# A graph layer's first stage, regrouped: blocks of 1536 nodes, the third vector component in four row groups, destinations loaded from a pool of their own

## The chip, the cores and the metric

The kernel runs on one core of a Trainium2 chip. The metric is device microseconds for one execution; before the change the runs took 5697.79 us in the median of three (5664.32 to 5704.07). One further execution was profiled; it took 4345.69 us, and the span from its first to its last instruction is 4343.6 us. Every time read from a view below is of that execution.

## What is computed

There are N = 12500 nodes with 160 features each: 64 scalars `s` and 32 vectors `v` of 3 components. There are 400000 edges, sorted by destination. Cut to what matters:

```python
h_s = s @ lin1_ws * a / sqrt(64)                                   # first stage: h, one row of 160 per node
h_v = einsum('nci,cd->ndi', v, lin1_wv) * a / sqrt(32)
w = silu(edge_scalars @ fc_w1 / 8) @ fc_w2 / 8                     # 224 weights per edge
es, ev = h_s[edge_src], h_v[edge_src]                              # gather
mid = products of w, es, ev and edge_attr                          # per edge
agg = segment_sum(mid, edge_dst) / 4                               # per destination
pre = sc(s, v) * a + agg @ lin2 * a                                # self connection, output map
out = layernorm(x + gated(silu / sigmoid of pre))
```

## The kernel before, in words

The program has five parts; each of the engines TensorE (PE), VectorE (DVE), ScalarE (ACT) and GpSimd (POOL) works through its own list of instructions in order, and SP and ACT also issue DMAs, each in its order.

**Setup (lines 99 to 120).** ACT issues the loads of `at` (node_vec1, 128 nodes to a column), of the 64x64 weight `l1s` (line 102) and of `l1v`, a 96x96 block-diagonal matrix with `lin1_wv` three times (lines 106 to 115). DVE scales both (lines 103 and 112). POOL fills the accumulator `acc`, 96x25088 numbers, with zeros (line 119).

**First stage (lines 122 to 149).** It computes h for all nodes into a table in DRAM, `h_tab`. Chunks of 1024 nodes: SP loads `xs` (64 partitions, line 129) and `xv` (96 partitions, one group of 32 for each vector component, line 131), three buffers of each. For each tile of 128 nodes PE makes two products, line 136 with 64 and line 137 with 96 rows of contraction; the node features are the stationary operand (128 columns) and the weights are the moving one (64 or 96 columns). A float32 product is two weight loads and two matmuls. The result goes to one of six PSUM buffers `hp`. DVE (even tiles, line 142) or ACT (odd tiles, line 140) multiplies by `at` into `ht`, and SP writes eight tiles with one DMA (line 146; line 149 for the rest of 84 nodes). The write stands in SP's list among the loads of later chunks.

**Destinations (lines 155 to 179).** `db` (line 157) and `dt` (line 160), two layouts of all destinations of 1.6 MB each, are loaded by ACT's queue. DVE takes the smallest and largest destination of each block of 640 edges (lines 162 and 163), ACT's queue writes them to DRAM (165) and reads them back in two layouts, `both` (167) and `lo` (170). DVE subtracts `lo` from `dt` to give `rel` (171), which the selections of the main loop compare with a ramp, and makes `rows` and `again`. The tiles of this part lie in a pool "ends" that takes the memory that the pool "nodes" of the first stage gives back, so its loads come after that stage has let its buffers go.

**Main loop (line 348 and those that lines 354 to 520 call).** 3125 tiles of 128 edges, four to a step. POOL gathers the rows of h (line 260, one indirect DMA to a tile), PE computes the edge weights (251, 272), DVE the products (280, 289) and the selection matrices (299, 302), PE sums by destination (318), ACT and PE turn and map the sums (322 to 343) and DVE adds them to `acc` (348). PE, DVE, ACT and POOL keep the order in which the code is written there. SP's loads (`es` line 239, `idx` 369, `eat` 371) lie in a pool "loads", opened at the loop and placed in memory that "nodes" and "ends" have given back.

**Last stage (from line 565).** Gates, residual and layernorm of the 98 tiles.

Outside the main loop the framework puts each engine's instructions into an order of its own, by what is ready and by the place in the code; the small weights of lines 195 to 231 (ACT's queue, some 50 loads) are spread in this way over the first stage. All DMAs share eight semaphores in turn.

Of the kernel before, what the change touches and what calls it, by code (L numbers as in the profile page):

```python
# [10 lines left out]
F32 = mybir.dt.float32  # L11
I32 = mybir.dt.int32
# [3 lines left out]
OP = mybir.AluOpType  # L16
AX = mybir.AxisListType
ENG = mybir.EngineType
PSUM = bass.MemoryType.PSUM

P = 128
S = 64
V = 32
V3 = 3 * V
D = S + V3
TB = 5
BG = 25
EB = TB * P
EG = BG * EB
W = 32  # L30
# [31 lines left out]
def gnn_kernel(  # L62
# [21 lines left out]
    nc = tc.nc  # L84
    N = x.shape[0]
    NT = attr.shape[1]
    NP = NT * P
    G = src.shape[0]
    NB = G * BG
# [3 lines left out]
    consts = ctx.enter_context(tc.tile_pool(name="consts", bufs=1))  # L93
    dram = ctx.enter_context(tc.tile_pool(name="dram", bufs=1, space=bass.MemoryType.DRAM))
    h_tab = dram.tile([N, D], F32, name="h_tab")
    bounds = dram.tile([2, NB], I32, name="bounds")


    at = consts.tile([P, NT], F32, name="at")
    nc.scalar.dma_start(at, attr)  # L100
    l1s = consts.tile([S, S], F32, name="l1s")
    nc.scalar.dma_start(l1s, lin1_ws)
    nc.vector.tensor_scalar_mul(l1s, l1s, 1.0 / math.sqrt(S))

    def block_diagonal(name, w, n, scale):
        k = w.shape[0]
        m = consts.tile([n * k, n * k], F32, name=name)
        nc.vector.memset(m, 0.0)
        for i in range(n):
            nc.scalar.dma_start(m[i * k:(i + 1) * k, i * k:(i + 1) * k], w)  # L110
        if scale != 1.0:
            nc.vector.tensor_scalar_mul(m, m, scale)
        return m

    l1v = block_diagonal("l1v", lin1_wv, 3, 1.0 / math.sqrt(V))


    acc = consts.tile([V3, 2, NP], F32, name="acc")
    nc.gpsimd.memset(acc, 0.0)


    with tc.tile_pool(name="nodes", bufs=3) as nodes, tc.tile_pool(
        name="nodes_ps", bufs=6, space=PSUM
    ) as nps:
        CH = 1024
        for c0 in range(0, N, CH):
            cn = min(CH, N - c0)
            xs = nodes.tile([S, CH], F32, name="xs")
            nc.sync.dma_start(xs[:, :cn], xs_t[:, c0:c0 + cn])
            xv = nodes.tile([V3, CH], F32, name="xv")  # L130
            nc.sync.dma_start(xv[:, :cn], xv_t[:, c0:c0 + cn])
            ht = nodes.tile([P, CH // P, D], F32, name="ht")
            for q in range(0, cn, P):
                n = min(P, cn - q)
                p = nps.tile([P, D], F32, name="hp")
                nc.tensor.matmul(p[:n, :S], xs[:, q:q + n], l1s, start=True, stop=True)
                nc.tensor.matmul(p[:n, S:], xv[:, q:q + n], l1v, start=True, stop=True)
                t = (c0 + q) // P
                if t % 2:
                    nc.scalar.mul(ht[:n, q // P], p[:n], at[:n, t:t + 1])  # L140
                else:
                    nc.vector.tensor_scalar(ht[:n, q // P], p[:n], at[:n, t:t + 1], None,
                                            op0=OP.mult)
            full = cn // P
            if full:
                nc.sync.dma_start(
                    h_tab[c0:c0 + full * P, :].rearrange("(q p) d -> p q d", p=P), ht[:, :full])
            if cn > full * P:
                nc.sync.dma_start(h_tab[c0 + full * P:c0 + cn, :], ht[:cn - full * P, full])


    rel = consts.tile([P, NB * TB], I16, name="rel")
    rows = consts.tile([1, NB], I32, name="rows")
    again = consts.tile([1, 1], I32, name="again")
    with tc.tile_pool(name="ends", bufs=1) as ends:
        db = ends.tile([G * BG // 5, 5, EB], I32, name="db")
        nc.scalar.dma_start(db.rearrange("a b e -> a (b e)"),
                            dst_b.rearrange("g (a e) -> (g a) e", e=5 * EB))
        dt = ends.tile([P, NB, TB], I32, name="dt")
        nc.scalar.dma_start(dt.rearrange("p b t -> p (b t)"), dst)  # L160
        mm = ends.tile([G * BG // 5, 2, 5], I32, name="mm")
        nc.vector.tensor_reduce(mm[:, 0], db, AX.X, OP.min)
        nc.vector.tensor_reduce(mm[:, 1], db, AX.X, OP.max)
        for k in range(2):
            nc.scalar.dma_start(bounds[k].rearrange("(a b) -> a b", b=5), mm[:, k])
        both = ends.tile([1, 2, NB], I32, name="both")
        nc.scalar.dma_start(both.rearrange("o k b -> o (k b)"),
                            bounds.rearrange("(o k) b -> o (k b)", o=1))
        lo = ends.tile([P, NB], I32, name="lo")
        nc.scalar.dma_start(lo, bounds[0:1, :].to_broadcast([P, NB]))  # L170
        nc.vector.tensor_tensor(rel.rearrange("p (b t) -> p b t", t=TB), dt,
                                lo[:, :, None].to_broadcast([P, NB, TB]), op=OP.subtract)

        nc.vector.tensor_copy(rows, both[:, 0])
        wide = ends.tile([1, NB], F32, name="wide")
        nc.vector.tensor_sub(wide, both[:, 1], both[:, 0])
        widest = ends.tile([1, 1], F32, name="widest")
        nc.vector.tensor_reduce(widest, wide, AX.X, OP.max)
        nc.vector.tensor_scalar(again, widest, float(W), float(G), op0=OP.is_ge, op1=OP.mult)


    ident = consts.tile([P, P], F32, name="ident")
# [14 lines left out]
    for half in range(2):  # L197
        r = slice(half * S, (half + 1) * S)
# [25 lines left out]
    for to, part, pieces, w, r0, c0, by in maps:  # L224
        for k, piece in enumerate(pieces):
# [3 lines left out]
            r = l2[at_r:at_r + V, m, c0:c0 + w.shape[1]]  # L229
# [124 lines left out]
            out.append([(half, u) for half in range(2) for u in range(t, t + 2) if u < sides[half]])  # L354
        return out

    with tc.tile_pool(name="loads", bufs=2) as loads, tc.tile_pool(
        name="edge", bufs=2
    ) as edge, tc.tile_pool(name="deep", bufs=4) as deep, tc.tile_pool(
        name="pw_ps", bufs=2, space=PSUM  # L360
    ) as pw_ps, tc.tile_pool(name="pa_ps", bufs=2, space=PSUM) as pa_ps, tc.tile_pool(
        name="misc_ps", bufs=2, space=PSUM
# [54 lines left out]
        for n, (_, _, tiles) in enumerate(steps):  # L417
            for t, _, _ in tiles:
                b = t // TB
# [110 lines left out]
        with tc.For_i(0, n_again, 1) as g, tc.For_i(0, BG, 1) as k:  # L530
            b = g * BG + k
# [4 lines left out]
            ends = loads.tile([1, 2], I32, name="ends1", bufs=1)  # L536
# [10 lines left out]
            r = edge.tile([P, TB], F32, name="r", bufs=1)  # L547
# [17 lines left out]
    with tc.tile_pool(name="fin", bufs=2) as fin, tc.tile_pool(  # L565
        name="fin_ps", bufs=4, space=PSUM
    ) as fps:
        full = N // P
# [3 lines left out]
        for t0, nt, p in groups:  # L572
# [5 lines left out]
            for t in range(nt):  # L578
                c = (t0 + t) * P
                a = at[:p, t0 + t:t0 + t + 1]  # L580
                pp = fps.tile([P, 2, V3], F32, name="pp")
                for k in range(2):
# [4 lines left out]
                                               op0=OP.mult, op1=OP.mult)  # L587
# [11 lines left out]
            for t in range(nt):  # L599
                nc.vector.tensor_scalar(y[:p, t], y[:p, t], mv[:p, t, 0:1], rs[:p, t:t + 1],  # L600
                                        op0=OP.subtract, op1=OP.mult)
# [47 lines left out]
```

## Time and profile before

| what | value |
|---|---|
| runs, median of three | 5697.79 us |
| profiled execution | 4345.69 us, span 4343.6 us |
| PE busy / DVE / ACT / POOL in the span | 3481.0 / 2620.0 / 749.0 / 3083.3 us |
| first matmul of the first stage | 21.85 us after the start |
| last product of the first stage ends | about 134.8 us |
| issue of the load of `db` | 137.49 us |
| first gather | 176.69 us |
| last gather | about 4190 us |

The profile gives, for each engine, what it did and when; "idle before" names the thing that ended a wait. A busy share is an average over stages with different limits, so the parts are read one by one, with the window of each. The profiled execution is shorter than the timed ones by 1352 us; a change of some us in one stage is worked out in the profiled execution and then set beside the median.

### The profile page before, as it was taken

How to read it: one execution, taken by the hardware profiler on the slowest of the kernel's cores; microseconds unless marked ns; L12 is line 12 of the kernel's file. 1: busy time of each engine (PE TensorE's matmuls, PEld its weight loads, DVE VectorE, ACT ScalarE, POOL GpSimd, SP SyncE). 2: the span in 40 equal slices, each digit the busy share in tenths (PEclk: the TensorE clock that was granted, in tenths of full speed). 3: DMA queues.
4: the chain of work that ended last, by engine and by line, in shares of the span. 5: the costliest groups of instructions: out<-in, count | busy, mean ns of one | idle time of the engine just before them, and what ended most of it. 6: DMA issues, size and time to landing. Idle time of an engine off the chain costs nothing. (4 is left out here: it accounts for less than half of the span.)

```text
span 4343.6 us, 90044 instructions
## 1 busy us (share of the span) xinstructions
PE 3481.0 (80%) x36179; PEld 2014.9 (46%) x36179; DVE 2620.0 (60%) x5738; ACT 749.0 (17%) x1662; POOL 3083.3 (71%) x3133
## 2 busy tenths in 40 slices
PE   6588888888888887788888888888878888888873
PEld 6344444444444444444444444444444444444442
DVE  3356666656666665666656566566656665566659
ACT  1111111111111111111111111111111111111124
POOL 2277777777777777777777777777777777777740
PEclk9999999999999999999999899999999999999975
DMA  4434433433334343433444333443443433433324
GB/s 113 124 91 102 95 92 93 101 91 94 95 91 100 94 95 91 101 95 89 96 99 94 91 95 92 97 97 93 96 98 92 96 93 94 99 93 88 92 74 118
DMA packets 231236, 416.33 MB, mean 96 GB/s; under 512 B 63556, under 2 KB 158544, under 8 KB 230561
## 3 DMA queue, kind: packets, MB, share of 16 engines
q0 software_dynamic: 150000, 256.20, 25.2%
q1 hardware_dynamic: 77622, 150.43, 13.8%
q8 instruction: 284, 4.65, 0.5%
q10 hardware_dynamic: 3192, 3.92, 0.4%
q14 instruction: 138, 1.13, 0.1%
HBM read 394.31 MB, written 16.00 MB: 94 GB/s over the span
## 5 line engine op out<-in xcount | busy, mean ns | idle before, releaser
L260 POOL DMA_INDIRECT hg<-h_tab,idx x3125 | 3061.5, 980 | 1105.9 <-issue 881.6
L318 PE MATMUL pa<-pr,sel 128*32 128x192 f32 x25000 | 1339.5, 355 | 548.3 <-DVE pr L289 543.0
L280 DVE TENSOR_TENSOR pr<-pw,hg 128x512 f32<-128x512 f32 x782 | 539.5, 690 | 1526.0 <-DMA hg<-h_tab,idx 1339.5
L318 PEld LDWEIGHTS pa<-pr,sel 128*32 128x32 f32 x25000 | 759.5, 116 | 997.5 <-DVE pr L289 676.8
L289 DVE TENSOR_TENSOR pr<-pw,hg 128x384 f32<-128x384 f32 x2346 | 1158.1, 549 | 10.5 <-issue 6.0
L272 PE MATMUL pw<-w,hid 64*128 64x224 f32 x6250 | 849.5, 392 | 0.7 <-ACT hid L253 0.7
L272 PEld LDWEIGHTS pw<-w,hid 64*128 64x128 f32 x6250 | 563.3, 197 | 440.4 <-issue 346.9
L302 DVE TENSOR_TENSOR sel<-oh,eat 128x640 f32<-128x640 f32 x625 | 517.3, 828 | 44.0 <-DVE oh L299 0.9
L251 PE MATMUL ph<-es,w 128*128 128x512 f32 x940 | 496.4, 612 | 44.6 <-DMA idx<-in_src_dram 40.8
L253 ACT ACTIVATE hid<-ph 128x512 f32<-128x512 f32 (+1 forms) x470 | 246.7, 525 | 962.4 <-PE ph L251 962.4
L322 ACT COPY sa<-pa 128x384 f32<-128x384 f32 x313 | 149.5, 478 | 1418.1 <-PE pa L318 1415.2
L339 PE MATMUL po<-tt,l 96*96 96x256 f32 (+1 forms) x1738 | 391.2, 381 | 0.0
L330 PE MATMUL pt<-ident,sa 128*96 128x128 f32 x1250 | 265.3, 294 | 148.3 <-ACT tt L331 148.3
L339 PEld LDWEIGHTS po<-tt,l 96*96 96x96 f32 x1738 | 275.4, 163 | 104.8 <-issue 22.4
L331 ACT COPY tt<-pt 96x256 f32<-96x256 f32 x626 | 229.8, 367 | 384.8 <-PE pt L330 383.3
L330 PEld LDWEIGHTS pt<-ident,sa 128*96 128x96 f32 x1250 | 107.6, 126 | 314.5 <-ACT tt L331 227.3
L251 PEld LDWEIGHTS ph<-es,w 128*128 128x128 f32 x940 | 151.1, 202 | 206.1 <-issue 181.7
L299 DVE TENSOR_TENSOR oh<-rel,iota 128x160 f32<-128x160 int16 x625 | 196.5, 314 | 0.0
L343 ACT COPY os<-po 96x512 f32<-96x512 f32 (+1 forms) x79 | 45.5, 577 | 599.2 <-PE po L339 599.2
L348 DVE TENSOR_TENSOR acc<-acc,os 96x64 f32 x625 | 133.3, 213 | 12.9 <-ACT os L343 7.9
L583 PE MATMUL pp<-ident,acc 96*128 96x96 f32 x196 | 53.0, 379 | 70.8 <-DVE y L588 37.1
L309 PE MATMUL pa<-none 1*128 1x384 bf16 x313 | 107.6, 344 | 0.0
(54 smaller groups left out, 681.9 us busy)
## 6 DMA issues: line engine op xcount, KB each, us to landing
es<-in_es_t_dram SPq DMA_DIRECT2D x312, 320.0 KB
hg<-h_tab,idx POOLq DMA_INDIRECT x3125
h_tab<-ht SPq DMA_DIRECT2D x12, 640.0 KB
xt<-in_x_dram SPq DMA_DIRECT2D x7, 1040.0 KB
out_dram<-y SPq DMA_DIRECT2D x7, 1040.0 KB
eat<-in_ea_dram SPq DMA_DIRECT2D x25, 250.0 KB
xv<-in_xv_t_dram SPq DMA_DIRECT2D x25, 187.5 KB
xv<-in_xv_t_dram SPq DMA_DIRECT2D x12, 384.0 KB
```

The costliest lines, as they stand in the source:

```text
L251: nc.tensor.matmul(ph[:k, c], w1[:k, :k], es[:k, t0 * P + c0 * P:t0 * P + c1 * P], start=True, stop=True)
L253: nc.scalar.activation(hid[:k, c], ph[:k, c], AF.Silu, scale=1.0 / math.sqrt(64))
L260: nc.gpsimd.indirect_dma_start(out=hg[:, t, :], out_offset=None, in_=h_tab, in_offset=bass.IndirectOffsetOnAxis(ap=i, axis=0))
L272: nc.tensor.matmul(pw[:, t, :NWT], hid[r, c * P:(c + 1) * P], w2[r], start=True, stop=True)
L280: nc.vector.tensor_mul(pr[:, :n, 6 * V:10 * V].rearrange("p t (k c) -> p t k c", k=2), pw[:, :n, :2 * S].rearrange("p t (k c) -> p t k c", ...
L289: nc.vector.tensor_mul(bass.AP(tensor=full.tensor, offset=full.offset, ap=[full.ap[0], full.ap[1], [step * V, 3], [1, V]]), pw[:, :n, None ...
L299: nc.vector.tensor_tensor(oh, r[:, :, None].to_broadcast([P, TB, W]), iota[:, None, :].to_broadcast([P, TB, W]), op=OP.is_equal)
L302: nc.vector.tensor_mul(sel, oh[:, :, None, :].to_broadcast([P, TB, 4, W]), e[:, :, :, None].to_broadcast([P, TB, 4, W]))
L318: nc.tensor.matmul(pa[k * W:(k + 1) * W], sel[:, t, k], a, start=start, stop=stop)
L330: nc.tensor.transpose(pt[:, half, b], sa[:, b, half * V3:(half + 1) * V3], ident)
L331: nc.scalar.copy(tt[:, half, :, at_b:at_b + nb].rearrange("c k b n -> c b k n"), pt[:, half, :nb].rearrange("c b (k n) -> c b k n", k=4))
L339: nc.tensor.matmul(po[:, k, :nb], l2[:, terms[to, part, half]], tt[:, half, part, :nb], start=(n == 0), stop=(n == len(of) - 1))
```

## The change

It does the following.

- **Blocks of 1536 nodes**, that is four quarters of three tiles. `xa` holds on 128 partitions the scalars (0 to 63) and the first two vector components (64 to 127), so one product of full contraction with the 128x128 block-diagonal `l1` gives 128 of the 160 columns. 12500 nodes make eight full blocks and a rest of 212, which is treated as one quarter of two tiles.
- **The third component in row groups.** `xz` holds it in four groups of 32 partitions, one for each quarter, with `lin1_wv` four times in `l1z`. For each of the three places in a quarter there come four products of 128 rows and then four of 32 rows, each of these in its own group of rows and its own PSUM bank.
- **PSUM and evictions.** A PSUM bank holds three tiles (480 columns), eight banks. DVE alone evicts, with one multiplication of 128x480 to a bank; ACT evicts nothing.
- **Queues.** SP issues only the loads (six for a block), ACT's queue writes h, once for a block.
- **Buffers.** "nodes" has two buffers in place of three. The pools "loads" and "ends" are opened ahead of the first stage, so they have memory of their own, and the loads of `db` and `dt`, unchanged in the code and still after the first stage in it, need no buffer of that stage.

The core of the diff (the body of the destinations' part is the same but for the name of its pool):

```diff
-    l1s = consts.tile([S, S], F32, name="l1s")
-    nc.scalar.dma_start(l1s, lin1_ws)
-    nc.vector.tensor_scalar_mul(l1s, l1s, 1.0 / math.sqrt(S))
+
+
+    l1 = consts.tile([P, P], F32, name="l1")
+    nc.vector.memset(l1, 0.0)
+    nc.scalar.dma_start(l1[:S, :S], lin1_ws)
+    for i in range(2):
+        r = slice(S + i * V, S + (i + 1) * V)
+        nc.scalar.dma_start(l1[r, r], lin1_wv)
+    l1z = consts.tile([P, V], F32, name="l1z")
+    for q in range(4):
+        nc.scalar.dma_start(l1z[q * V:(q + 1) * V], lin1_wv)
+    nc.vector.tensor_scalar_mul(l1[:S], l1[:S], 1.0 / math.sqrt(S))
+    nc.vector.tensor_scalar_mul(l1[S:], l1[S:], 1.0 / math.sqrt(V))
+    nc.vector.tensor_scalar_mul(l1z, l1z, 1.0 / math.sqrt(V))
 
     def block_diagonal(name, w, n, scale):
...
-    l1v = block_diagonal("l1v", lin1_wv, 3, 1.0 / math.sqrt(V))
...
-    with tc.tile_pool(name="nodes", bufs=3) as nodes, tc.tile_pool(
-        name="nodes_ps", bufs=6, space=PSUM
-    ) as nps:
-        CH = 1024
-        for c0 in range(0, N, CH):
-            cn = min(CH, N - c0)
-            xs = nodes.tile([S, CH], F32, name="xs")
-            nc.sync.dma_start(xs[:, :cn], xs_t[:, c0:c0 + cn])
-            xv = nodes.tile([V3, CH], F32, name="xv")
-            nc.sync.dma_start(xv[:, :cn], xv_t[:, c0:c0 + cn])
-            ht = nodes.tile([P, CH // P, D], F32, name="ht")
-            for q in range(0, cn, P):
-                n = min(P, cn - q)
-                p = nps.tile([P, D], F32, name="hp")
-                nc.tensor.matmul(p[:n, :S], xs[:, q:q + n], l1s, start=True, stop=True)
-                nc.tensor.matmul(p[:n, S:], xv[:, q:q + n], l1v, start=True, stop=True)
-                t = (c0 + q) // P
-                if t % 2:
-                    nc.scalar.mul(ht[:n, q // P], p[:n], at[:n, t:t + 1])
-                else:
-                    nc.vector.tensor_scalar(ht[:n, q // P], p[:n], at[:n, t:t + 1], None,
-                                            op0=OP.mult)
-            full = cn // P
-            if full:
-                nc.sync.dma_start(
-                    h_tab[c0:c0 + full * P, :].rearrange("(q p) d -> p q d", p=P), ht[:, :full])
-            if cn > full * P:
-                nc.sync.dma_start(h_tab[c0 + full * P:c0 + cn, :], ht[:cn - full * P, full])
...
-    with tc.tile_pool(name="ends", bufs=1) as ends:
...
+    loads = ctx.enter_context(tc.tile_pool(name="loads", bufs=2))
+    ends = ctx.enter_context(ExitStack())
+    ends_pool = ends.enter_context(tc.tile_pool(name="ends", bufs=1))
+
+
+    U = 3
+    with tc.tile_pool(name="nodes", bufs=2) as nodes, tc.tile_pool(
+        name="nodes_ps", bufs=8, space=PSUM
+    ) as nps:
+        CH = 4 * U * P
+        for c0 in range(0, N, CH):
+            cn = min(CH, N - c0)
+            quarters = 4 if cn == CH else 1
+            assert quarters == 4 or cn <= U * P
+            cq = cn // quarters
+            xa = nodes.tile([P, CH], F32, name="xa")
+            nc.sync.dma_start(xa[:S, :cn], xs_t[:, c0:c0 + cn])
+            nc.sync.dma_start(xa[S:, :cn], xv_t[:2 * V, c0:c0 + cn])
+            xz = nodes.tile([P, U * P], F32, name="xz")
+            for q in range(quarters):
+                nc.sync.dma_start(xz[q * V:(q + 1) * V, :cq],
+                                  xv_t[2 * V:, c0 + q * cq:c0 + (q + 1) * cq])
+            ht = nodes.tile([P, 4 * U, D], F32, name="ht")
+            ps = [nps.tile([P, U, D], F32, name="hp") for _ in range(quarters)]
+            for u in range(-(-cq // P)):
+                n = min(P, cq - u * P)
+                for q in range(quarters):
+                    e = q * cq + u * P
+                    nc.tensor.matmul(ps[q][:n, u, :P], xa[:, e:e + n], l1, start=True, stop=True)
+                for q in range(quarters):
+                    r = slice(q * V, (q + 1) * V)
+                    nc.tensor.matmul(ps[q][:n, u, P:], xz[r, u * P:u * P + n], l1z[r],
+                                     start=True, stop=True)
+            full = cn // P
+            for q in range(quarters):
+                t = c0 // P + q * U
+                k = min(U, full - q * U)
+                nc.vector.tensor_mul(ht[:, q * U:q * U + k], ps[q][:, :k],
+                                     at[:, t:t + k, None].to_broadcast([P, k, D]))
+            nc.scalar.dma_start(
+                h_tab[c0:c0 + full * P, :].rearrange("(q p) d -> p q d", p=P), ht[:, :full])
+            if cn > full * P:
+                n = cn - full * P
+                t = c0 // P + full
+                nc.vector.tensor_scalar(ht[:n, full], ps[0][:n, full], at[:n, t:t + 1], None,
+                                        op0=OP.mult)
+                nc.scalar.dma_start(h_tab[c0 + full * P:c0 + cn, :], ht[:n, full])
+
+
+    db = ends_pool.tile([G * BG // 5, 5, EB], I32, name="db")
+    nc.scalar.dma_start(db.rearrange("a b e -> a (b e)"),
+                        dst_b.rearrange("g (a e) -> (g a) e", e=5 * EB))
+    dt = ends_pool.tile([P, NB, TB], I32, name="dt")
...
+    ends.close()
...
-    with tc.tile_pool(name="loads", bufs=2) as loads, tc.tile_pool(
+    with tc.tile_pool(
```

More of the change, by code (lines that the diff above doesn't have):

```diff
@@ L154, in gnn_kernel @@
     again = consts.tile([1, 1], I32, name="again")
-    with tc.tile_pool(name="ends", bufs=1) as ends:
[L156 to L179, printed above, removed]
@@ new lines, in gnn_kernel @@
+    db = ends_pool.tile([G * BG // 5, 5, EB], I32, name="db")
+    nc.scalar.dma_start(db.rearrange("a b e -> a (b e)"),
+                        dst_b.rearrange("g (a e) -> (g a) e", e=5 * EB))
+    dt = ends_pool.tile([P, NB, TB], I32, name="dt")
+    nc.scalar.dma_start(dt.rearrange("p b t -> p (b t)"), dst)
+    mm = ends_pool.tile([G * BG // 5, 2, 5], I32, name="mm")
+    nc.vector.tensor_reduce(mm[:, 0], db, AX.X, OP.min)
+    nc.vector.tensor_reduce(mm[:, 1], db, AX.X, OP.max)
+    for k in range(2):
+        nc.scalar.dma_start(bounds[k].rearrange("(a b) -> a b", b=5), mm[:, k])
@@ new lines, in gnn_kernel @@
+    both = ends_pool.tile([1, 2, NB], I32, name="both")
+    nc.scalar.dma_start(both.rearrange("o k b -> o (k b)"),
+                        bounds.rearrange("(o k) b -> o (k b)", o=1))
+    lo = ends_pool.tile([P, NB], I32, name="lo")
+    nc.scalar.dma_start(lo, bounds[0:1, :].to_broadcast([P, NB]))
+    nc.vector.tensor_tensor(rel.rearrange("p (b t) -> p b t", t=TB), dt,
+                            lo[:, :, None].to_broadcast([P, NB, TB]), op=OP.subtract)
+    nc.vector.tensor_copy(rows, both[:, 0])
@@ L182, in gnn_kernel @@
+    wide = ends_pool.tile([1, NB], F32, name="wide")
+    nc.vector.tensor_sub(wide, both[:, 1], both[:, 0])
+    widest = ends_pool.tile([1, 1], F32, name="widest")
+    nc.vector.tensor_reduce(widest, wide, AX.X, OP.max)
+    nc.vector.tensor_scalar(again, widest, float(W), float(G), op0=OP.is_ge, op1=OP.mult)
+    ends.close()
     ident = consts.tile([P, P], F32, name="ident")
```

## The prediction

> **What bounds the kernel now.** I read the table of busy time by window first. Columns after the length: busy us of PE, weight loads, DVE, ACT, POOL (counts), granted clock, DMA share, GB/s.
>
> ```profile
> 0.00:22.00 22.00, 0.15 (x1) 0.15 (x1) 18.30 (x8) 1.28 (x1) 21.44 (x6) 1.00 0.43 97
> 22.00:138.00 116.00, 100.27 (x392) 88.83 (x392) 22.91 (x73) 19.26 (x49) 0.39 (x2) 1.00 0.46 124
> 138.00:177.00 39.00, 1.38 (x2) 0.50 (x2) 12.33 (x7) 1.28 (x1) 0.31 (x1) 1.00 0.48 126
> 177.00:4204.00 4027.00, 3325.91 (x35589) 1896.83 (x35588) 2443.07 (x5047) 671.31 (x1487) 3061.20 (x3125) 0.94 0.40 94
> ```
>
> The edited part is 22 to 177 us. The 4027 us of the main loop keep their code, so the most that can be had is 155 us. PE fills the first stage; in the 39 us after it every engine waits. The timeline of setup and stage shows what PE is made of:
>
> ```profile
> 0.75 21.00 POOL L119 MEMSET acc<- 96x25088 f32 x1 [0.29 <-POOLq L637]
> 5.08 16.72 DVE L103 TENSOR_SCALAR l1s<-l1s 64x64 f32<-64x64 f32 x1 [2.54 <-DMA l1s<-in_lin_ws_dram]
> 24.60 2.63 PEld L137 LDWEIGHTS hp<-l1v,xv 96*128 96x128 f32 x12
> 28.69 0.50 PEld L136 LDWEIGHTS hp<-l1s,xs 64*128 64x128 f32 x2 [0.17 <-issue]
> 28.69 0.69 PE L136 MATMUL hp<-l1s,xs 64*128 64x64 f32 x2
> 29.30 0.50 PEld L137 LDWEIGHTS hp<-l1v,xv 96*128 96x128 f32 x2
> 29.30 0.74 PE L137 MATMUL hp<-l1v,xv 96*128 96x96 f32 x2
> 29.97 2.21 PEld L136 LDWEIGHTS hp<-l1s,xs 64*128 64x128 f32 x10 [0.17 <-issue]
> ```
>
> Twelve weight loads start within 2.63 - 0.33 us: one per 0.21 us, at 96 as at 64 moving columns, so the load of 128 columns paces. A lone tile has four loads but lasts 29.97 - 28.69 = 1.28 us; 1.28 - 4 x 0.21 = 0.44 us goes to two changes between 64- and 96-row products, 0.22 each. The scaling of l1s lasts until POOL's memset ends at 21.75 us. The timeline after the stage:
>
> ```profile
> 135.45 0.50 SPq L149 DMA_DIRECT2D h_tab<-ht  x1
> 137.49 0.50 ACTq L157 DMA_DIRECT2D db<-in_dst_b_dram  x1
> 155.41 3.49 DVE L162 TENSOR_REDUCE mm<-db 125x5 int32<-125x3200 int32 x1 [20.45 <-DMA db<-in_dst_b_dram]
> 164.65 3.42 DVE L171 TENSOR_TENSOR rel<-dt,lo 128x3125 int16<-128x3125 int32 x1 [2.35 <-DMA lo<-bounds]
> 170.24 1.12 SPq L239 DMA_DIRECT2D es<-in_es_t_dram  x2
> 176.69 1.10 POOL L260 DMA_INDIRECT hg<-h_tab,idx  x1 [154.27 <-DMA eat<-in_ea_dram]
> ```
>
> A chain: h written, buffers free (137.5), db loaded (155.4), bounds out and back, rel, ends free (170.2), es, idx and eat loaded, first gather 176.69. In the waits up to 200 us, `PE hp L136 <- DMA xs` takes 12.5 us in two pieces: loads queued behind writes on SP.
>
> [...] The 64x128 loads average 321 ns in this stage and 197 ns at line 272, so I take the stage to be at half clock although the table prints 1.00. [...] No four row groups are in the trace[...]:
>
> ```profile
> 190.80 1.51 PE L318 MATMUL pa<-pr,sel 128*32 128x192 f32 x32
> ...
> 192.87 1.03 PE L272 MATMUL pw<-w,hid 64*128 64x224 f32 x8
> ```
>
> 32 products of 0.35 us in 1.51 us, 8 of 0.39 us in 1.03. [...]
>
> **The change part by part**, in the profiled execution.
>
> 1. *Start.* Eight small DMAs in place of five on ACT's queue ahead of at most 21 us of waiting: hidden by POOL's memset. If it were not, 3 x 0.5 us. Three scalings instead of two on DVE, all ending just behind the memset. PE starts at 22 us as before.
>
> 2. *PE.* For each place in the quarters, four tiles: 8 loads for the full products at 0.21 = 1.68 us; 8 in the row groups, four at a time, 2 x 0.21 = 0.42; two changes 0.44. Sum 2.54 us for four tiles, against 4 x 1.28 = 5.12 for lone tiles. 24 places: 61 us; the rest of two tiles at 1.28: 3. Sum 64 us, against 113 (21.85 to 134.8). Bounds of the unknown: all at full clock, loads at half, 64 - 25 = 39 us, and then the DMAs pace (point 3); row groups one after another, 8 x 0.21 instead of 0.42, 24 x 1.26 = 30 us more. I take overlap at half clock.
>
> 3. *DMAs of the stage.* 16 MB (12500 x 160 x 4 x 2). The window 22 to 138 has 124 GB/s at a share of 0.46, so 270 GB/s if full: 59 us, of which the loads of two blocks (2 MB, 7 us) come before 22. 52 stands below 64 and beside it. db and dt add 3.1 MB, 12 us, issued while PE still waits for the memset. Since SP no longer waits for evictions, loads run one block ahead (7.6 us of PE against 1 MB, 3.7 us). All DMAs share eight semaphores in turn, so some wait for another queue's; before, waits on xs cost 12.5 us. I allow 5, between 0 and 20.
>
> 4. *Evictions.* DVE 128x384 takes 549 ns and 128x512 takes 690, so 128x480 is 0.655; 32 of them, 21 us, the same as the 23 of DVE now. Hidden by PE and eight banks (two blocks); uncovered, the last four cost 2.6 us. DVE's list is in order too: where rel or a minimum waits for its DMA ahead of an eviction, PE runs on for one block, 7.6 us, before it stops; that is part of the 5 us of point 3. ACT loses 19 us of work nobody waited for.
>
> 5. *h on ACT's queue.* Ten issues of 0.4 us. An issue waits for DVE; behind it stand the small weights, db, dt and the four transfers of bounds, for which rel and the first step of the loop wait, all needed only after h. SP is relieved of a wait of 83.5 us in all for DVE.
>
> 6. *Destinations.* Their loads wait for no buffer. The order outside the loop follows readiness (weights written later in the code are loaded earlier now), so I take them to be issued in the first 30 us. DVE's 3.49 + 3.48 + 3.42 + 2.2 = 12.6 us and the scalings of weights (5) bring it to 39 us of the 64: hidden. If the cover failed, the 39 us come back, since the first selection (line 302) reads rel and all DVE work of the loop stands behind it.
>
> 7. *Loads of the loop.* es, idx and eat no longer wait for ends; SP issues them after its last block, under the tail.
>
> Sum: 22 + 64 + 5 for waits + 2.7 from the last product to h landed (134.8 to 137.49 now) = 94 us for the first gather, instead of 176.69: 83 us less. The first gather shifts everything after it; the loop is as long as before. 4345.7 - 83 = 4263 for the profiled execution.
>
> **Against the median.** It is 1352 us above the profiled execution, and no view shows where. An estimate: the stage is at half clock already, while the loop is mostly at full clock; an execution with more half clock lengthens the loop and not this stage. So 83 us are carried over whole: 5697.8 - 83 = 5615. If everything were stretched alike, by 1.31, it would be 109: 5589.
>
> **Rivals.** *Row groups one after another* ([...]no four row groups in the trace): 30 us back, 53 saved, 5645. *DMAs pace*: six loads a block, two buffers, shared semaphores. At the 161 GB/s of the busiest 20 us before, a block of 1.97 MB takes 12.2 us; eight make 98, first gather near 126, 51 saved, 5647. Against: SP's waits for evictions made those 161. *Destinations stay behind* on ACT's queue, after the last h, as the code has them: 39 us come back, 44 saved, 5654. In this case the change does not do what it says. *Slower*: the clock granted in the loop. The loop's 0.94 over 4027 us is 483 us at half clock; each microsecond more of it costs at most half. Beyond 166 us more the gain is gone, and at 300 more it ends at 5697.8 - 83 + 150 = 5765. For: 4346 against 5698 says that executions differ; against: three runs lie within 40 us and the loop's code is the same.
>
> **Numbers.** Chances: the sum above 0.62, row groups 0.11, DMAs 0.12, destinations 0.08, slower clock 0.05, a gain over 109 us by the clock 0.02. The likeliest is 5615. Its own range is 5585 to 5635; with the rivals that save 44 to 53 us, and 0.35% of spread between runs, 5575 to 5660. One per cent (57 us) is about what a measurement of this kernel can tell from no change: faster takes the first case nearly whole, the last and a tenth of the middle ones, 0.70; the same 0.24; slower 0.06.
>
> **What would show it.** Right: first gather near 94 us; loads of row groups starting four together; db landed before 45 us and rel made before the last h; PE waiting for no load after the first block. Wrong: products of row groups 0.21 us apart (rival one), PE idle for xa or xz (two), db issued after the last h (three). The prediction falls if the first gather comes after 120 us, or if the loop's length moves by more than 25 us.

## The result, and the profile after

| what | before | after |
|---|---|---|
| runs, median (four each) | 5690.96 us | 5618.01 us |
| ratio, 95% interval | | 0.9875 [0.9832, 0.9917] |
| profiled execution, its span | 4345.69, 4343.6 us | 5611.19, 5609.4 us |
| products of the first stage | 21.8 to 134.8 us | 22.1 to 109.6 us |
| issue of the load of db | 137.5 us | 5.6 us |
| rel made | from 164.6 us | from 47.0 us |
| first gather | 176.7 us | 115.9 us |

The forecast was 5615 us. The two profiled executions are not comparable in the main loop: the chips used for this study take between 4339 and 5842 us for the same kernel before, with a granted clock of 0.93 to 0.82. So the stages are compared by their own times, and the loop by a second profile of the kernel before, at a clock of 0.82 (first experiment). The table by window of the changed kernel, columns as before:

```profile
0.00:22.00 22.00, 0.00 (x0) 0.00 (x0) 17.96 (x8) 0.00 (x0) 21.43 (x6) 1.00 0.79 172
22.00:110.00 88.00, 83.84 (x392) 69.46 (x392) 35.74 (x67) 0.00 (x0) 0.39 (x2) 0.71 0.73 190
116.00:5449.00 5333.00, 4055.29 (x35379) 2125.17 (x35383) 2437.36 (x5023) 660.59 (x1476) 3029.16 (x3124) 0.83 0.27 71
```

The 39 us without work are gone, and the first stage lasts 88 us in place of 113, not the 64 and 5 of the forecast. PE is busy 83.84 of the 88, so it looks as if PE paced. Its timeline, with the other lines that answer to those of before (line 160 is the product of 128 rows, 163 that of 32):

```profile
5.57 0.75 ACTq L182 DMA_DIRECT2D db<-in_dst_b_dram  x1
...
47.03 3.40 DVE L196 TENSOR_TENSOR rel<-dt,lo 128x3125 int16<-128x3125 int32 x1
...
91.93 2.08 PE L160 MATMUL hp<-l,xa 128*128 128x128 f32 x8
93.93 0.65 PE L163 MATMUL hp<-l1z,xz 32*128 32x32 f32 x8
...
97.75 0.80 PE L160 MATMUL hp<-l,xa 128*128 128x128 f32 x2
98.48 0.63 PE L163 MATMUL hp<-l1z,xz 32*128 32x32 f32 x2
99.04 0.80 PE L160 MATMUL hp<-l,xa 128*128 128x128 f32 x2
...
115.87 1.10 POOL L286 DMA_INDIRECT hg<-h_tab,idx  x1 [93.47 <-issue]
```

At 91.93 a place is as the code has it: the eight matmuls of its four full products start within 2.00 us, and the eight matmuls of the row groups need about 0.6 us (a float32 product is two matmuls: 392 for the 196 products of the stage). From 97.75 on the tiles stand one by one, 99.04 - 97.75 = 1.29 us each, as before the change. The framework put PE's list into an order of its own here; some 28 of the 96 tiles of full blocks stand so.

### The profile page after: what moved, and what is told of

Same layout as the page of the kernel before. It is cut to its first block, busy times and chain, and to the rows that moved or that the text cites. A ratio compares the mean times of both kernels' runs of the same rounds, so it can differ in the third digit from the quotient of the medians.

```text
span 5609.4 us, 89958 instructions
## 1 busy us (share of the span) xinstructions
PE 4213.3 (75%) x36179; PEld 2236.0 (40%) x36179; DVE 2623.9 (47%) x5724; ACT 721.9 (13%) x1612; POOL 3052.1 (54%) x3133
## 5 line engine op out<-in xcount | busy, mean ns | idle before, releaser
L286 POOL DMA_INDIRECT hg<-h_tab,idx x3125 | 3030.2, 970 | 2397.4 <-DVE pr L315 940.7
L344 PE MATMUL pa<-pr,sel 128*32 128x192 f32 x25000 | 1830.0, 387 | 380.0 <-issue 366.9
L344 PEld LDWEIGHTS pa<-pr,sel 128*32 128x32 f32 x25000 | 890.9, 125 | 1156.4 <-issue 896.7
L298 PE MATMUL pw<-w,hid 64*128 64x224 f32 x6250 | 993.1, 426 | 39.3 <-issue 33.4
L356 PE MATMUL pt<-ident,sa 128*96 128x128 f32 x1250 | 315.7, 342 | 834.2 <-ACT tt L357 335.5
L298 PEld LDWEIGHTS pw<-w,hid 64*128 64x128 f32 x6250 | 640.5, 216 | 573.0 <-issue 515.9
L277 PE MATMUL ph<-es,w 128*128 128x512 f32 x940 | 537.1, 656 | 15.3 <-issue 13.8
L356 PEld LDWEIGHTS pt<-ident,sa 128*96 128x96 f32 x1250 | 121.0, 142 | 1028.5 <-ACT tt L357 404.9
L365 PE MATMUL po<-tt,l 96*96 96x256 f32 (+1 forms) x1738 | 417.7, 392 | 14.3 <-issue 13.2
L277 PEld LDWEIGHTS ph<-es,w 128*128 128x128 f32 x940 | 162.9, 215 | 196.5 <-issue 184.7
L335 PE MATMUL pa<-none 1*128 1x384 bf16 x313 | 116.9, 373 | 1.1 <-issue 1.1
```

What stands on the lines that cost most here:

```text
L277: nc.tensor.matmul(ph[:k, c], w1[:k, :k], es[:k, t0 * P + c0 * P:t0 * P + c1 * P], start=True, stop=True)
L286: nc.gpsimd.indirect_dma_start(out=hg[:, t, :], out_offset=None, in_=h_tab, in_offset=bass.IndirectOffsetOnAxis(ap=i, axis=0))
L298: nc.tensor.matmul(pw[:, t, :NWT], hid[r, c * P:(c + 1) * P], w2[r], start=True, stop=True)
L344: nc.tensor.matmul(pa[k * W:(k + 1) * W], sel[:, t, k], a, start=start, stop=stop)
L356: nc.tensor.transpose(pt[:, half, b], sa[:, b, half * V3:(half + 1) * V3], ident)
L365: nc.tensor.matmul(po[:, k, :nb], l2[:, terms[to, part, half]], tt[:, half, part, :nb], start=(n == 0), stop=(n == len(of) - 1))
```

## Experiments

Below, "products end" is the end of the last matmul of the first stage. A run that was taken once has no interval.

**The kernel before once more, and the parts.** The first four ran on one chip, on which the kernel before takes 5694 us.

> The kernel before, unchanged, profiled once more and timed against itself. Theory (the gain is the earlier start of the main loop, nothing else): the first gather starts at 176.7 us within 2 us whatever the loop's clock is; ratio 1.000 within 0.004. If this execution is granted the clock of the changed kernel's profile (0.82 in place of 0.93), the span is about 5690 us and the loop from first gather to last stage about 5340 us, as in the changed kernel (5344 from 116 to 5460). Rival (the first stage runs at another clock in such an execution, so the 83 us were worked out from the wrong stage): the first gather is later than 180 or earlier than 170 us.

Measured: 1.0014 [0.9996, 1.0033]; span 5704.3 us; first gather at 176.0 us.

```profile
176.00:5544.00 5368.00, 4041.14 (x35377) 2122.81 (x35375) 2437.26 (x5022) 659.66 (x1475) 3026.93 (x3124) 0.82 0.29 71
```

The loop, from the first gather to the last, in the first profile:

```profile
177.00:4189.00 4012.00, 3312.12 (x35457) 1887.33 (x35456) 2439.58 (x5035) 668.77 (x1480) 3060.37 (x3125) 0.94 0.40 94
```

The loop is 1356 us longer than in the first profile of the same kernel, and what comes ahead of it is the same to 0.7 us. So the step that carried the gain over to the median whole, and not stretched, held. Beside the loop of the changed kernel (5333) it shows 35 us more; the three other variants on this chip have 5340 to 5347, so a loop of one execution is known to some 20 or 30 us only.

```diff
+    loads = ctx.enter_context(tc.tile_pool(name="loads", bufs=2))
+    early = ctx.enter_context(ExitStack())
+    ends = early.enter_context(tc.tile_pool(name="ends", bufs=1))
     with tc.tile_pool(name="nodes", bufs=3) as nodes, tc.tile_pool(
...
-            ht = nodes.tile([P, CH // P, D], F32, name="ht")
+            ht = nodes.tile([P, CH // P, D], F32, name="ht", bufs=2)
```

> The kernel before with one part of the change: the pools of the loop's loads and of the destinations opened ahead of the first stage (ht with two buffers in place of three, to fit the memory). Theory (the chain after the stage is 39 us and goes whole): the stage ends at 135 us as before, the first gather starts at 139 to 142 us, 35 to 38 us earlier, ratio 0.9935. Rival (the loads of 3.1 MB and their chain on ACT, which also evicts, push the stage back by what they save): first gather after 155 us, ratio above 0.996.

Measured (the rest of this edit moves the destinations' code out of its block): 0.9923 [0.9899, 0.9946], 44.5 us less; first gather at 134.6 us, 41.4 earlier.

```profile
134.57 1.10 POOL L263 DMA_INDIRECT hg<-h_tab,idx  x1 [112.15 <-DMA eat<-in_ea_dram]
```

The chain goes, as the theory has it: from the last product to the first gather it is 6.7 us in place of 41.7. The rest of the 41.4 is the stage's own, which ends at 127.9, 6.4 us earlier than before and outside the forecast. PE waits there 1.4 us in place of 12.0 and is busy 104.5 in place of 100.5; why its loads came sooner was not tried. So the chain costs the stage nothing.

In the changed kernel, "ends" opened behind the first stage and "loads" at the loop:

```diff
-    loads = ctx.enter_context(tc.tile_pool(name="loads", bufs=2))
-    ends = ctx.enter_context(ExitStack())
-    ends_pool = ends.enter_context(tc.tile_pool(name="ends", bufs=1))
     U = 3
...
+    ends = ctx.enter_context(ExitStack())
+    ends_pool = ends.enter_context(tc.tile_pool(name="ends", bufs=1))
     db = ends_pool.tile([G * BG // 5, 5, EB], I32, name="db")
...
-    with tc.tile_pool(
+    with tc.tile_pool(name="loads", bufs=2) as loads, tc.tile_pool(
```

> The changed kernel with the pools where they were: first stage and queues as changed, the destinations' tiles and the loop's loads in memory that the first stage gives back. Theory (the two parts add up): h is complete near 108 to 113 us, a chain of 39 us follows, the first gather comes at 150 to 155 us, 22 to 27 us earlier than before, ratio 0.995 to 0.996. Rival (loading the destinations beside it is what lengthens the changed stage, so without them it takes about 70 us): first gather at 130 to 140 us, ratio 0.992 to 0.993.

Measured: 0.9924 [0.9897, 0.9951], 37.6 us less by the medians; first gather at 153.6 us, 22.4 earlier; products end at 109.0 us.

```profile
153.64 1.10 POOL L285 DMA_INDIRECT hg<-h_tab,idx  x1 [131.24 <-DMA eat<-in_ea_dram]
```

By the trace the parts add up: 41.4 + 22.4 = 63.8, and both together 60.1 (176.0 - 115.9). The runs gained 15 us more than the first gather moved, so the ratio is below the forecast. The rival falls: without db and dt the stage is as long.

The whole first stage of the changed kernel, moved in under one line:

```diff
+    with tc.manual_schedule(engines={ENG.PE}):
         U = 3
```

> The changed kernel with PE's order in the first stage held as the code has it: four products of 128 rows, then four of 32 rows in their four row groups, in every block. Theory (the stage came out 22 us longer than forecast because about half of its tiles stand one by one in PE's list, 1.28 us each, and not four together, 2.58 us for four): all 24 places take 2.6 us, the stage takes 64 to 70 us, the first gather comes at 94 to 99 us in place of 116, and the ratio to before is 0.984 to 0.986. Rival (the stage is paced by its loads, which wait for other queues' transfers): PE's idle time grows by what the grouping saves, and the first gather stays at 112 to 118 us.

Measured: 0.9888 [0.9864, 0.9911]; products end at 106.6 us, first gather at 114.7 us. My theory of the missing 22 us falls as it was put, and what the rival said has come. All 24 places are compact in PE's list, 2.00 + 0.58 us where nothing is late, but PE then waits:

```profile
22.00:107.00 85.00, 69.50 (x392) 60.94 (x392) 35.89 (x67) 0.00 (x0) 0.39 (x2) 0.56 0.75 197
```

PE is busy 69.5 of 85 us, in place of 83.84 of 88. Of its waits 11.2 us end with a load of xa or xz and 3.8 with an eviction. Where the loads are late is seen in the timeline of this kernel (lines are one higher):

```profile
29.92 1.71 SPq L153 DMA_DIRECT2D xz<-in_xv_t_dram  x4
29.92 3.49 DVE L188 TENSOR_REDUCE mm<-db 125x5 int32<-125x3200 int32 x1 [7.48 <-DMA db<-in_dst_b_dram]
...
33.33 2.34 DVE L170 TENSOR_TENSOR ht<-hp,at 128x480 f32<-128x480 f32 x4
...
36.31 1.38 PE L164 MATMUL hp<-l1z,xz 32*128 32x32 f32 x8 [3.89 <-DMA xz<-in_xv_t_dram]
```

The loads of xz for the second block are issued at 29.92, in the moment in which db has landed; the first minimum stands on DVE ahead of the first evictions. SP's waits in the changed kernel (us in all, times, longest) name the same:

```profile
SPq L152 <- DMA db<-in_dst_b_dram: 18.5, 1, 18.5
SPq L152 <- DMA l<-in_lin_wv_dram: 9.7, 3, 5.2
SPq L152 <- DMA w<-in_fc_w_dram: 9.2, 3, 4.8
SPq L152 <- DMA h_tab<-ht: 9.1, 2, 6.6
```

No load of xz needs db. In the trace of the changed kernel the 543 DMAs of SP and ACT share eight semaphores (the 3125 gathers have eight others), and the first load of xz for the second block, issued at 29.14 us, carries the one that db had at 5.57.

**Two limits, one behind the other.** If the lone tiles and the late loads each hide the other, removing both must show it. The next four ran on a chip where the kernel before takes 4339 us.

> The first stage as changed with PE's order held as the code has it, and the pools where they were before the change, so that the destinations are loaded after the stage. Theory (two limits lie one behind the other: the lone tiles in PE's list, and the load of db, which runs until 29 us and on whose semaphore a load of the second block waits for 19 us; each hides what the removal of the other saves): with both gone the stage's products end at 88 to 96 us in place of 109, and the first gather comes at 132 to 141 us in place of 153.6. Rival (the rate of the block loads, with two buffers, paces the stage): the products still end at 104 to 110 us.

Measured (its edit is the last two together; 35 us less in one run): products end at 94.7 us, first gather at 139.7, both as the theory forecast. The four combinations give the end of the products:

| | PE's order by the framework | by the code |
|---|---|---|
| destinations beside the stage | 109.6 | 106.6 |
| after the stage | 109.0 | 94.7 |

Each change alone moves it by 3.0 or 0.6 us, both by 14.9. But the four executions were not granted the same clock. The clock records hold two values alone, 1.0 and 0.5 (246 of each in the changed kernel). By them PE had full clock in this stage for 3.4 us in the other three and for 13.7 us here:

```profile
32.08 1.16 PE L158 MATMUL hp<-l,xa 128*128 128x128 f32 x8
33.17 0.42 PE L161 MATMUL hp<-l1z,xz 32*128 32x32 f32 x8
33.52 1.16 PE L158 MATMUL hp<-l,xa 128*128 128x128 f32 x8
```

A place takes 33.52 - 32.08 = 1.44 us then in place of 2.58, so a microsecond of work at full clock saves 0.79. Here PE worked 10.3 us at full clock, which saves at most 8.1; in the other three it saves at most 1.3 to 2.5 (a lone tile takes 0.75 us at full clock). If all of this reached the end, an estimate of the four at half clock throughout is 112.1 and 107.9, 111.5 and 102.8: each change alone 4.2 or 0.6, both 9.3. That the two limits hide each other stays, but its size is not shown to better than this. It is also not the 86 of the forecast: PE is busy 59.8 of 73 us here, and xa and xz are waited for 12.7 us, mostly behind writes of h and small weights on the shared semaphores (SP waits 25.8 us for h and 12.1 for weights).

```diff
-    nc.scalar.dma_start(db.rearrange("a b e -> a (b e)"),
-                        dst_b.rearrange("g (a e) -> (g a) e", e=5 * EB))
+    rows_of = dst_b.rearrange("g (a e) -> (g a) e", e=5 * EB)
+    for a0, a1 in ((0, 112), (112, G * BG // 5)):
+        nc.scalar.dma_start(db[a0:a1].rearrange("a b e -> a (b e)"), rows_of[a0:a1])
```

> The changed kernel with PE's code order, and the load of db cut into 112 and 13 partitions in place of 125 in one piece. Theory ([...]what waits for its semaphore waits so much less): db is complete before 20 us, the wait of a block load for db is gone or below 5 us, the products end at 92 to 98 us in place of 106.6, first gather at 98 to 105 us. Rival (the rate of all DMAs paces): the products end at 104 to 108 us.

Measured: 56 us less in one run; products end at 101.9 us, between the two forecasts, first gather at 110.8. db's packets run from 7.0 to 15.0 us in place of 6.9 to 28.5; the waits of block loads for db go from 19.4 to 4.4 us. The end of the products comes 4.7 us earlier, less than expected: now other transfers hold the block loads (small weights 20 us of SP's waits in all, h 8.4), and PE's waits are 16.5 us in place of 14.9. PE also worked 9.9 us at full clock here in place of 1.7, which saves up to 6.5 us, so that the cut of db shortens the stage at all is not shown. In one piece five of db's packets are under way at once for 14.3 of its 21.6 us, in two pieces sixteen are the most common number. How much of the shorter load is due to that is not shown, for dt runs beside db in the first case and is issued at 16.7 us, after it, in the second.

The lines from `ident` to `terms` (181 to 232 of the kernel before), moved ahead of these:

```diff
     acc = consts.tile([V3, 2, NP], F32, name="acc")
     nc.gpsimd.memset(acc, 0.0)
```

> As the run with db in two pieces, and in addition the small weights of the later stages (some 50 loads, with their scalings) written ahead of the first stage, so that they are issued while PE waits for the memset and take no semaphore between the block loads; the loads of db and dt fall between the writes of h by this. Theory (waits for shared semaphores: 20 us of SP's waits named small weights): first gather at 94 to 100 us, ratio 0.984. Rival (the waits named the small weights only because they came last; the rate paces): first gather within 3 us of the run with db in two pieces alone.

Measured: 0.9852 [0.9838, 0.9865], 65.0 us less; products end at 96.2 us, first gather at 108.1 us. By the first gather, which is what was forecast, the rival holds: 2.6 us earlier. The products end 5.7 us earlier; PE worked 15.2 us at full clock in place of 9.9, which is worth up to 4.2 of them. rel is now made from 92.5 us on and stands closer to the end. For the rival speaks also that the DMAs are full from 40 to 80 us (share 1.07 and 1.06):

```profile
40.00:60.00 20.00, 15.15 (x86) 13.40 (x86) 5.04 (x10) 0.00 (x0) 0.00 (x0) 0.50 1.07 296
60.00:80.00 20.00, 16.56 (x130) 14.56 (x129) 11.49 (x10) 0.00 (x0) 0.00 (x0) 0.76 1.06 304
```

```diff
-    nc.vector.tensor_scalar_mul(l1[:S], l1[:S], 1.0 / math.sqrt(S))
-    nc.vector.tensor_scalar_mul(l1[S:], l1[S:], 1.0 / math.sqrt(V))
-    nc.vector.tensor_scalar_mul(l1z, l1z, 1.0 / math.sqrt(V))
+    nc.scalar.mul(l1[:S], l1[:S], 1.0 / math.sqrt(S))
+    nc.scalar.mul(l1[S:], l1[S:], 1.0 / math.sqrt(V))
+    nc.scalar.mul(l1z, l1z, 1.0 / math.sqrt(V))
```

> As the run with db in two pieces, and the three scalings of the first weights on ACT in place of DVE, where they wait for the end of the memset at 21.8 us. Theory (PE's start is held by that alone): the first product starts at 8 to 12 us; as the loads then pace more than PE, the products end 4 to 12 us earlier than in the run with db in two pieces, first gather at 90 to 100 us, ratio 0.983 to 0.985. Rival (the loads pace from the start): the products end at the same time as in that run.

Measured: 0.9835 [0.9820, 0.9850], 68.5 us less; first product at 7.9 us, products end at 93.8 us, first gather at 104.1, 4 us after the forecast's range.

```profile
7.06 0.31 ACT L112 ACTIVATE l<-l 64x128 f32<-64x128 f32 x1
7.57 0.31 ACT L113 ACTIVATE l<-l 64x128 f32<-64x128 f32 x1 [0.20 <-DMA l<-in_lin_wv_dram]
7.93 2.07 PE L161 MATMUL hp<-l,xa 128*128 128x128 f32 x8 [7.93 <-DMA l1z<-in_lin_wv_dram]
```

On ACT a scaling takes 0.31 us beside POOL's memset; on DVE it took 16.3. Of the 14 us of earlier start 8 arrive at the end, though PE had less full clock than in the run with db in two pieces (3.6 us of work in place of 9.9): PE now waits 17.8 us, for xa and xz. Shift (176.7 - 104.1 = 72.6) and runs (68.5) agree within the interval.

**Row groups, the queue of h, and the repeat.** The last four ran on a chip where the kernel before takes 5842 us.

> The changed kernel, unchanged, profiled once more and timed. Theory (the gain is a shift of the loop's start that does not depend on the clock granted in the loop): first gather at 116 us within 2 us, the runs 58 to 64 us below the kernel before; on a chip whose runs of the kernel before take 4340 us that is a ratio of 0.985 to 0.987, on one with 5690 us 0.989. Rival (the clock of the loop makes the gain): another shift, or another difference, on a chip with another time of the kernel before.

Measured: 0.9886 [0.9871, 0.9902], 71 us less by the medians and 67 by the ratio; first gather at 119.5 us. Only the ratio is as the theory forecast. The first gather is 3.5 us later than in the first profile (the products end at 113.4; PE waits 8.1 us in place of 3.5), and the runs gained 71 us where it moved 56.5 (against the 176.0 of the other chip). The rival is not excluded by this.

```diff
-            xz = nodes.tile([P, U * P], F32, name="xz")
+            xz = nodes.tile([V, CH], F32, name="xz")
...
-                    nc.tensor.matmul(ps[q][:n, u, P:], xz[r, u * P:u * P + n], l1z[r],
+                    nc.tensor.matmul(ps[q][:n, u, P:], xz[:, e:e + n], l1z[:V],
```

> As the run of the first stage alone in code order (destinations after the stage), but the third component of all four quarters lies in one group of 32 rows, with as many loads, so that its products can't overlap. Theory (row groups save 24 x 1.26 = 30 us of PE): the eight products of a place take 1.9 us in place of 0.58, PE is busy without a break, and the products end at 115 to 125 us in place of 94.7. Rival (products of one group are pipelined so closely, or the loads pace so much, that groups save little): the products end before 105 us.

Measured: products end at 116.9 us in place of 94.7, first gather at 160.4, as the theory forecast; one run, 17 us below the kernel before.

```profile
24.14 1.91 PE L161 MATMUL hp<-l1z,xz 32*128 32x32 f32 x8
25.98 2.08 PE L158 MATMUL hp<-l,xa 128*128 128x128 f32 x8
```

The eight small matmuls take 25.98 - 24.14 = 1.84 us in place of 0.58: this is the 1.26 of the forecast's rival, and 24 times 1.26 is 30 us. PE is now busy 94.7 of 95 us, 35 more than in the run with row groups: 30 by the groups, while the rest goes with the clock, which was half here throughout. The stage grows by 22 only, because the 13 us in which PE had waited for loads are used up.

```diff
-            nc.scalar.dma_start(
+            nc.sync.dma_start(
                 h_tab[c0:c0 + full * P, :].rearrange("(q p) d -> p q d", p=P), ht[:, :full])
...
-                nc.scalar.dma_start(h_tab[c0 + full * P:c0 + cn, :], ht[:n, full])
+                nc.sync.dma_start(h_tab[c0 + full * P:c0 + cn, :], ht[:n, full])
```

> The changed kernel with h written by SP's queue in place of ACT's. Theory (an issue of h waits on SP for the evictions, and the loads of the block after next stand behind it): PE waits for xa or xz rise by 5 to 20 us and the first gather comes at 120 to 135 us in place of 116. Rival (loads wait for shared semaphores on either queue): first gather at 112 to 119 us.

Measured: products end at 150.6 us, first gather at 156.4, 40.5 us later than in the changed kernel (36.9 later than its repeat on this chip) and well beyond what the theory gave; one run, 31 us below the kernel before and 40 above the changed one. SP's timeline shows a period of 17.4 us to a block:

```profile
80.34 0.39 SPq L171 DMA_DIRECT2D h_tab<-ht  x1
80.82 3.12 SPq L152 DMA_DIRECT2D xz<-in_xv_t_dram  x4
84.04 0.47 SPq L148 DMA_DIRECT2D xa<-in_xs_t_dram  x1
84.56 0.59 SPq L149 DMA_DIRECT2D xa<-in_xv_t_dram  x1
97.76 0.39 SPq L171 DMA_DIRECT2D h_tab<-ht  x1
```

After the loads SP waits 12.6 us for the evictions of a block before it issues h, and the loads of xz for the next block stand behind. In these 12.6 us PE works through the block, mostly in lone tiles of 1.29 us: the framework gave PE another list for this edit, with some 55 lone tiles in place of 28. Against the repeat PE is busy 16.7 us longer and waits 20.7 longer, so that up to 17 of the 37 us come by way of PE's order, which the edit was not meant to touch. The stage in big blocks with h on SP's queue is longer than before the change (150.6 against 134.3).

> Code order on PE, db in two pieces, small weights written ahead of the first stage and the scaling of the first weights on ACT. Theory (the two gains of weights ahead and of the early start add up in part): the first product starts at 8 us, the products end at 84 to 92 us, first gather at 94 to 102 us, ratio 0.981 to 0.983 where the kernel before takes 4340 us. Rival (the small weights stand on ACT ahead of the first writes of h, so the early start is lost): first gather at 103 us or later, no better than the scaling on ACT alone.

Measured: 0.9859 [0.9840, 0.9878], 83 us less than the kernel before, 12 less than the changed kernel on the same chip; first product at 7.7 us, products end at 88.8 us, first gather at 101.0. This is the earliest first gather of all variants, and these three times are as the theory forecast. Beside the scaling on ACT alone the products end 5 us earlier, but PE also worked 13.2 us at full clock in place of 3.6, worth up to 7.6 us; that the two gains add up is therefore not shown.

## Why the prediction was right, and where its steps were not

**The shift of the loop's start: right.** The chain after the stage (41.7 to 6.7 us from the last product to the first gather) and the shorter stage were each measured alone, and together they give what the changed kernel gives. The profile ahead of the loop is the same at both clocks (176.7 and 176.0 us), so carrying the gain over whole, and not stretched, held too. The reason given for it holds in part only. The loop of the second profile of the kernel before is 1356 us longer than that of the first, and PE is busy 729 us longer in it (4041 against 3312). The clock records show some 1420 us more at half clock, of which the prediction, by its own estimate, counted at most half as lost. In the first stage a place takes 1.44 us at full clock and 2.58 at half, so 0.44 of the time at half clock is lost there. What the other half is stays open.

**The number: near by luck.** The forecast of the first gather, 94 us, was 22 us too early, and the shift 60.8 in place of 83. The runs gained 73 us [47, 96], 12 more than the shift, so 5618 came to stand beside 5615. On the slower chips all eight measurements (two of them single runs) gained more in the runs than the first gather moved, by 1 to 15 us, and on the chip of 4339 us all four gained less, by 2 to 10. There the loop itself, from the first gather to the last, is as long as before (4009 to 4017 us against 4012 in the first profile). Whether the loop gains some us on the slower chips, or single profiled executions differ by as much, is left open.

**Where the 22 us are.** In the forecast's own terms: 22 + 64 + 5 + 2.7 = 94, and in the changed kernel 22.1 + 83.8 + 3.5 + 6.3 = 115.7.

*PE: the price was right, the count was not.* A place costs 2.58 us (2.54 forecast). That four row groups overlap was the author's estimate from lines 272 (two halves of the rows) and 318 (four column groups); here their eight matmuls take 0.58 us, in one group 1.84, and the 1.26 us saved at each place are the rival's price. But the step "24 places" took the code's order for PE's. Some 28 lone tiles at 1.29 - 0.645 us are 18 us, nearly all of the 20 that PE is busy longer than 64.

*Waits: 3.5 us, within the allowance of 5, but only because PE was slow.* Loads wait behind transfers that they don't need (longest 18.5 us, behind db); with PE's order mended PE stands 15 of 85 us, between the 12.5 of before and the 20 of the upper bound. The two terms cover each other, so the mended PE term alone brings 3 us.

*The tail: 2.7 us forecast, 6.3 measured* (109.6 to 115.9). The 2.7 us of the forecast ran to the issue of db in the kernel before, not to a gather. Here the last three writes of h are issued between 109.7 and 111.0, among idx, eat and es, with the DMAs at a share of 0.82 from 110 to 116 us.

**h on ACT's queue: not priced.** I gave ten issues of 0.4 us and a relief; without this edit the stage of the changed kernel is 37 us longer (150.6 against 113.4 in the repeat), up to 17 of them by PE's order, and longer than before the change.

**The rivals and the signs.** Row groups one after another did not happen, and the run with one group shows what it would have been. The destinations did not stay behind (db issued at 5.6 us, landed before 29; rel made from 47). The loads paced in part. The loop was not slower. Two of the signs named for a right forecast did not come: the first gather near 94 us, and no wait of PE for a load after the first block. The loop's length moved by 35 us (5333 against 5368), more than the 25 that were to count against the prediction; the other variants on that chip, 5340 to 5347, make this the spread of single executions rather than the change, as far as is known.

Two sums of the prediction are off. The rival of the DMAs (22 + 98 + 2.7) gives a first gather near 123, not 126; and the parts of the 0.70 for "faster" make 0.67 at most.

## What to carry to other kernels

When an edit depends on the order of instructions on one engine, read or fix that engine's list; the order of the code is not it (some 28 of 96 tiles stood alone here), and an edit elsewhere can change it (some 55 with h on SP's queue). Two limits of similar length hide each other until both are removed (4.2 or 0.6 us for each alone, 9.3 for both, by the estimate above). Loads that are ready early should not share a queue with stores that wait for compute (the stage ended at 150.6 us in place of 113.4, up to 17 us of it by PE's order), nor their completion semaphores with one slow transfer (18.5 us of SP's waits were for db). A load can land sooner in pieces: the one on 125 partitions took 21.6 us whole, beside dt, and 8.0 us as 112 and 13 partitions, ahead of dt. A setup step that lasts as long as another engine's memset can be moved to an engine on which it does not, as the scaling here from DVE (16.3 us) to ACT (0.31 us). And before two profiles of one stage are compared, compare the clock that each was granted in it (a place took 2.58 us at half clock and 1.44 us at full).

## What was not expected of the hardware

- The clock printed as 1.00 is not full clock ahead of the first record (at 55.1 us in the changed kernel). With one row group the table prints 1.00 for the whole stage, and the eight matmuls of four full products take the same 2.00 us as in the run in code order at 80.4 us, where it prints 0.50. The forecast's reading (half clock) is borne out.
- In the same stage one execution has no full clock at all and another 20.5 us of it (one row group; small weights first). A full-clock place takes 1.44 us, one at half clock 2.58.
- 1.6 MB on 125 partitions take 21.6 us beside the block loads and dt, with mostly five packets under way at once; as 112 and 13 partitions 8.0 us beside the block loads, with up to sixteen and more.
- The same kernel takes 4339, 5694 and 5842 us on three chips, with granted clocks of 0.93, 0.83 and 0.82. The lower clock goes with the longer time, but between the last two it falls by less than 0.01 while the time grows by 148 us, so it is hardly the whole cause.
